# Two feed-forward blocks and an attention of a two-layer transformer: from token blocks of one batch to pairs of batches

## The chip, the cores and the metric

The kernel runs on one core of a Trainium2 chip. The metric is the device time of one execution in microseconds, as a median over runs. The engines that the text names are PE (matrix products, with PEld for its weight loads), DVE (elementwise work on vectors), ACT (elementwise functions and copies), POOL or GpSimd (elementwise work) and SP (issues DMA transfers). Each engine works through its own queue of instructions in order; semaphores make an instruction wait for one on another engine. Matrix results land in PSUM banks (128 partitions x 512 fp32), everything else is in SBUF.

## The reference

There are 4 batches of 256 tokens with 256 features, in fp32, and four residual steps, each on a layer norm of `x`:

```python
x = x + L0_attn(layernorm(x))   # 16 heads, 8 kv heads, rms norm + rope on q and k, window of 128
x = x + L0_ffn(layernorm(x))    # below
x = x + L1_attn(layernorm(x))   # 16 heads of 128, causal softmax, output projection W_O
x = x + L1_ffn(layernorm(x))    # silu(x W1) * (x W3), Walsh-Hadamard transform, then W2

# L0_ffn, hidden width 1024
h = silu(x @ w_gate) * (x @ w_up)
h_sparse = h with, of each 4 neighbours along the hidden axis, the 2 of largest |h| kept
out = h_sparse @ w_down
```

## The kernel before

Four stages follow each other on the core. In the trace the first attention takes 0 to 279 us, the first FFN 279 to 372, the second attention 372 to 655, and the second FFN 655 to the end at 737.2. A scheduler of the framework fixes the order of instructions on every engine when the program is built; tile pools (with a tag and a number of buffers each) decide when a buffer may be written again, and `tc.issue_after` puts an instruction behind another one.

**First FFN** (`ffn0`, `gated`, `keep_two_of_four`, `down`). Eight units: batch `b`, half `gc` of the hidden width. A unit has 16 plain matmuls (L550; 2 weights x 4 hidden blocks x 2 chunks of the contraction) with 256 moving columns, the batch's tokens. ACT applies Silu to the gate's PSUM tile (L556), DVE multiplies by up (L557, out of PSUM), ACT takes Abs (L530), and DVE builds the mask of the two largest and applies it (`keep_two_of_four`, L569 to L583, 256 columns wide, on bf16 counts). The down matmuls (L595) of a unit are issued two units later; the last two units' downs are done inside the second attention (`finish_ffn0`).

**Seven-product scheme** (`seven_products`, `left_of`, `right_of`). In the second attention's q, k and v projections and the second FFN's gate and up, a product of 2x2 blocks is made with seven block products instead of eight. `left_of` forms four sums of the blocks of x on DVE, `right_of` four sums of the blocks of the weights. The products come in the order 5, 1, 2, 6, 3, 7, 4 into PSUM tiles x, y, z: ACT copies the results of 5, 1 and 6 to SBUF (`u`), DVE adds c11 after 2, c12 after 3, c22 after 7 (three-way sums that use a `u`), and ACT copies c21 after 4. The lines that carry this:

```python
product(x, 6, False)
nc.scalar.copy(u[2], x)
product(y, 3, False)
nc.vector.tensor_tensor(c12, y, u[2], ALU.add)
```

Before the change the two left blocks are the two blocks of 128 tokens of one batch, so the moving operand of q, k, gate and up has 128 columns.

**Second attention** (`attention1`, `project1`, `pipelined`). 16 units of four heads (group `g`) and one batch. `pipelined` runs the stages project (unit n), score (n - 1) and attend (n - 2) in one step, and after them what `behind` holds for that step. A unit has 28 matmuls of 128 columns for q and k (L783) and 7 of 256 for v (L789), scores (L213, L214), the softmax, then GpSimd normalizes (`p`, L234) and splits it into 16-bit planes (`pl`, L240), a DMA transposes the planes (`plT`), ACT and DVE copy them together (`pT`, L260), and PE multiplies with v (`av`, L268, L271); ACT copies the result to `zT`. The output projection of unit n (`po`, L280) is behind step n + 3 for the first nine units; outputs 9, 10, 11 and 13 are `kept` and issued between the products of units 14 and 15's steps, 12 is at step 15, 14 and 15 at step 17. `load_group1` loads a group's weights by four DMAs on SP and forms `t_qk` and `t_v` on DVE; groups 0 and 1 are loaded ahead of the first FFN.

**Second FFN** (`ffn1`, `gated1`, `factors_ffn1`). Eight units of one batch and half of the hidden width, 28 matmuls of 128 columns (L858) and 8 downs of 256 of the unit before, which `between` puts among the products; `factors_ffn1` forms the weights' sums on DVE.

**Norms** (`normed`). With `by_dma` DVE makes `xn` (L171), GpSimd splits it into planes (`xpl`), a DMA on SP transposes them (`xplT`), and ACT joins them to `xnT` (L195).

## Time and profile before

| | |
|---|---|
| Median of 3 runs | 738.72 us (738.62 to 738.83) |
| Profiled execution, first to last instruction | 737.2 us |
| Median less that span | 1.5 us |
| Busy | PE 725.0, DVE 469.2, ACT 406.9, POOL 345.0 us |
| Granted PE clock | 1.00 over the span |

The profile is of one execution. The page gives the busy time of each engine, the chain of waits that ended last, and groups of instructions by source line: `Lnnn engine operation out<-in, partitions x elements, type, xcount | busy us, mean ns of one | idle us before them and what ended it`. The table by stage gives for a stretch of time the busy time (and count) of PE, PEld, DVE, ACT and POOL, the granted clock, the DMA share and GB/s. The timeline gives start, length, engine, line, operation and count; a bracket holds the idle time before and its releaser. Each fp32 matmul appears as two records, and the records of neighbouring matmuls overlap, so the rate of issue is read from the starts.

### The profile page before, as it was taken

How to read it: one execution, taken by the hardware profiler on the slowest of the kernel's cores; microseconds unless marked ns; L12 is line 12 of the kernel's file. 1: busy time of each engine (PE TensorE's matmuls, PEld its weight loads, DVE VectorE, ACT ScalarE, POOL GpSimd, SP SyncE). 2: the span in 40 equal slices, each digit the busy share in tenths (PEclk: the TensorE clock that was granted, in tenths of full speed). 3: DMA queues.
4: the chain of work that ended last, by engine and by line, in shares of the span. 5: the costliest groups of instructions: out<-in, count | busy, mean ns of one | idle time of the engine just before them, and what ended most of it. 6: DMA issues, size and time to landing. Idle time of an engine off the chain costs nothing.

```text
span 737.2 us, 11593 instructions
## 1 busy us (share of the span) xinstructions
PE 725.0 (98%) x3912; PEld 594.6 (81%) x3912; DVE 469.2 (64%) x1402; ACT 406.9 (55%) x983; POOL 345.0 (47%) x489
## 2 busy tenths in 40 slices
PE   9999999999999999999999999999999999999998
PEld 5556576666666778888898999999998999899997
DVE  6999878888887537987655644464442655464443
ACT  2487887667767952222355555555556576434332
POOL 1588878897799631011116433343336575520000
PEclk9999999999999999999999999999999999999999
DMA  8732344425445545001324532342232223401100
GB/s 327 293 64 51 57 93 81 92 52 93 90 79 96 77 114 180 16 14 26 119 72 77 127 55 44 70 129 46 44 72 44 44 44 44 88 15 22 23 14 30
DMA packets 138348, 57.51 MB, mean 78 GB/s; under 512 B 131504, under 2 KB 133680, under 8 KB 137520
## 3 DMA queue, kind: packets, MB, share of 16 engines
q1 hardware_dynamic: 138288, 56.77, 33.9%
q8 instruction: 31, 0.51, 0.3%
q14 instruction: 29, 0.24, 0.1%
HBM read 22.94 MB, written 1.05 MB: 33 GB/s over the span
## 4 chain that ended last, share of the span: by engine, by line
PE 75%; DVE 9%; POOL 7%; issue 4%; ACT 3%; DMA 2%; SPq 0%; POOLq 0%; DVEq 0%; ACTq 0%
PE pj L446 10%; PE pgu L550 7%; PE po L292 7%; PE po_f L595 7%; PE qk_x L783 5%; PE po L280 5%; PE sc L214 5%; PE gu_x L858 4%; PE av L394 3%; PE qk_y L783 3%; PE v_x L789 3%; PE sc L213 3%; PE av L268 2%; POOL p L234 2%; PE gu_y L858 2%
## 5 line engine op out<-in xcount | busy, mean ns | idle before, releaser
L234 POOL TENSOR_SCALAR p<-p,rs 128x128 f32<-128x128 f32 (+1 forms) x256 | 115.4, 470 | 153.2 <-DVE rs L231 147.9
L240 POOL TENSOR_SCALAR pl<-p 128x1536 uint16<-128x1536 uint16 x64 | 94.3, 1474 | 4.8 <-POOL p L234 0.5
L260 ACT COPY pT<-plT 128x1536 uint16<-128x1536 uint16 (+1 forms) x60 | 86.2, 1494 | 11.5 <-DMA plT<-pl 11.5
L216 DVE CUSTOM_DVE_ANT_0 p<-sc,cst 128x128 f32<-128x128 f32 (+1 forms) x256 | 79.7, 351 | 10.5 <-PE sc L214 8.1
L226 ACT ACTIVATE p<-p,nb,r 128x128 f32<-128x128 f32 (+1 forms) x128 | 68.2, 535 | 20.2 <-DVE nb L223 20.2
L446 PE MATMUL pj<-wq,xnT 128*128 128x512 f32 x128 | 61.1, 595 | 1.1 <-DVE qT L508 1.1
L446 PE MATMUL pj<-wkv,xnT 128*128 128x512 f32 x128 | 60.1, 592 | 0.0
L226 ACT ACTIVATE p<-p,nb 128x128 f32<-128x128 f32 (+1 forms) x128 | 56.3, 447 | 4.0 <-DVE nb L221 4.0
L292 PE MATMUL po<-wo,zT 128*128 128x256 f32 x256 | 57.9, 379 | 0.0
L280 PE MATMUL po<-w_o,zT 128*128 128x256 f32 x256 | 57.6, 379 | 0.0
L456 ACT ACTIVATE sq<-pj 128x512 f32<-128x512 f32 (+1 forms) x64 | 30.9, 489 | 42.7 <-DVE qc L451 42.4
L292 PEld LDWEIGHTS po<-wo,zT 128*128 128x128 f32 x256 | 48.3, 190 | 7.0 <-ACT kT L519 0.6
L280 PEld LDWEIGHTS po<-w_o,zT 128*128 128x128 f32 x256 | 47.7, 190 | 6.0
L156 POOL TENSOR_SCALAR ve<-mv 128x2 f32<-128x2 f32 (+1 forms) x17 | 4.3, 253 | 97.5 <-DVE mv L152 97.0
L446 PEld LDWEIGHTS pj<-wkv,xnT 128*128 128x128 f32 x128 | 24.3, 190 | 30.2 <-issue 28.0
L451 DVE TENSOR_TENSOR qs<-pj,sin_s 128x512 f32<-128x512 f32 (+1 forms) x64 | 35.3, 551 | 13.5 <-PE pj L446 12.9
L446 PEld LDWEIGHTS pj<-wq,xnT 128*128 128x128 f32 x128 | 23.5, 190 | 24.2 <-issue 19.9
L666 ACT COPY qk<-qk_x 128x512 f32<-128x512 f32 x16 | 9.4, 587 | 58.1 <-PE qk_x L783 58.1
L268 PE MATMUL av<-pT,v 128*128 128x256 f32 x128 | 38.4, 382 | 1.2 <-DVE nb L221 1.1
L214 PE MATMUL sc<-kT,qT 128*128 128x256 f32 x128 | 38.3, 381 | 0.0
L214 PE MATMUL sc<-qk 128*128 128x256 f32 x128 | 38.2, 380 | 0.0
L240 POOL TENSOR_SCALAR qpl<-qc 128x1024 uint16<-128x1024 uint16 x20 | 28.8, 1453 | 18.9 <-PE av L398 8.2
(151 smaller groups left out, 1748.8 us busy)
## 6 DMA issues: line engine op xcount, KB each, us to landing
w<-in_w_dram SPq DMA_DIRECT2D x3, 1024.0 KB, 4.7
wq<-in_wq_dram SPq DMA_DIRECT2D x4, 512.0 KB, 7.6
wkv<-in_wkv_dram SPq DMA_DIRECT2D x4, 512.0 KB, 8.4
wo<-in_wo_dram SPq DMA_DIRECT2D x4, 512.0 KB, 10.2
w_qk<-in_w_q_dram SPq DMA_DIRECT2D x4, 512.0 KB, 5.2
w_qk<-in_w_k_dram SPq DMA_DIRECT2D x4, 512.0 KB, 6.1
w_v<-in_w_v_dram SPq DMA_DIRECT2D x4, 512.0 KB, 7.3
w_o<-in_w_o_dram SPq DMA_DIRECT2D x4, 512.0 KB, 6.0
```

What stands on the lines that cost most here:

```text
L214: nc.tensor.matmul(sc[:, P : 3 * P], lhsT=q[:, P:T], rhs=k, start=True, stop=True)
L216: last_of["mx"] = nc.vector.tensor_tensor_reduce(out=p[:, j, cols], in0=sc[:, cols], in1=mask[:, cols], scale=1.0, scalar=-3.0e38, op0=ALU ...
L226: last_of["exp"] = nc.scalar.activation(p[:, j, cols], p[:, j, cols], AF.Exp, bias=nb[:, j, i : i + 1], scale=SCALE1 if rq is None else rq ...
L234: nc.gpsimd.tensor_scalar(p[:, j, cols], p[:, j, cols], rs[:, j, i : i + 1], 1.0, ALU.mult, ALU.mult)
L240: last_of["planes"] = nc.gpsimd.tensor_scalar(o, i, 1.0, 1.0, ALU.mult, ALU.mult)
L260: copy(words.rearrange("p (n w) -> p w n", w=2), halves[:, :, js].rearrange("p w j n -> p w (j n)"),)
L268: nc.tensor.matmul(av, lhsT=v0, rhs=pT[:, 0:T], start=True, stop=False, skip_group_check=True)
L280: nc.tensor.matmul(po[:, t, :], lhsT=zT[:, j, t * P : (t + 1) * P], rhs=w[:, j, :], start=(t == j == 0), stop=(j == 3), skip_group_check=True,
L292: nc.tensor.matmul(po, lhsT=zTs[hd // 4][:, hd % 4, t * P : (t + 1) * P], rhs=w[:, hd, :], start=(hd == 0), stop=(hd == n - 1),)
L446: last_of[0] = nc.tensor.matmul(pj, lhsT=xnT[:, c, t * P : (t + 1) * P], rhs=w[:, g, c, :], start=(c == 0), stop=(c == NC - 1),)
L550: nc.tensor.matmul(o[:, j, :], lhsT=w[:, c, f0 + j, :], rhs=xnT[:, c, :], start=(c == 0), stop=(c == NC - 1),)
L783: last_of[1] = nc.tensor.matmul(o[:, j, :], lhsT=wqk[i - 1][:, j // 2, j % 2, :], rhs=x[i - 1], start=(first and j == 0), stop=True, skip_ ...
```

## The change

Batches are taken in pairs from the first FFN on. The seven-product schemes take the two batches of a pair, rather than the two token blocks of a batch, as the rows of the left blocks: `left_of` gets two normed batches, and the moving operands have 256 columns. A unit of the second attention is then a group, a pair and a half `a` of its heads; v is made per token block `a`. The output projection of a batch needs two `zT` and stands one step later (n + 4); 13 moves to step 15, outputs 14 and 15 become fill of the second FFN's first unit.

The first FFN's gate and up are made by the scheme, in 4 units of 28 matmuls, by the same `gated` that the second FFN now uses; `factors` for it runs on GpSimd. Gate and up are SBUF tiles of the tag "qk" (2 buffers). The product h is made on GpSimd per batch, Abs on ACT per batch, and `keep_two_of_four` is 512 columns wide. The first `load_group1` is issued after the third unit, with its sums on GpSimd; the others follow in the second attention. Pools are split by stage: `work0`, `work1`, `work2`; the first FFN's norm planes have 4 buffers, h 2, a and counts 1, and `st` has 4 PSUM banks from the first FFN on.

The core of the diff:

```diff
+    def norm_planes(shape, name):
+        if in_ffn0:
+            return work.tile(shape, U16, tag="npl", name=name, bufs=4)
+        return page_of_planes(shape, name)
...
-    def project_out1(po, zT, w, b):
+    def project_out1(po, heads, w, b):
 
         for t in range(NT):
-            for j in range(4):
+            for j, zT in enumerate(heads):
                 nc.tensor.matmul(
-                    po[:, t, :], lhsT=zT[:, j, t * P : (t + 1) * P], rhs=w[:, j, :],
+                    po[:, t, :], lhsT=zT[:, t * P : (t + 1) * P], rhs=w[:, j, :],
                     start=(t == j == 0), stop=(j == 3), skip_group_check=True,
                 )
-        for t in range(NT):
+                if j % 2:
+                    yield
...
+    def factors(half, w_g, w_u, engine):
+
+        t = late.tile([P, 2, 4, 2, P], F32, tag="qkt", name="t_gu")
+        r = []
+        for i, w in enumerate((w_g, w_u)):
+            w = w[:, :, 4 * half : 4 * half + 4, :].rearrange("p c (a m) f -> p c a m f", m=2)
+            r.append(right_of(*(w[:, c, :, m, :] for c in range(2) for m in range(2)),
+                              [t[:, i, k] for k in range(4)], engine))
+        return r
+
+    def gated(x, r, gate_at, up_at, between):
+
+        def chain(w, o):
+            def product(ps, i, first):
+                for j in range(2):
+                    nc.tensor.matmul(
+                        ps[:, j, :], lhsT=w[i - 1][:, j, :], rhs=x[i - 1],
+                        start=(first and j == 0), stop=True, skip_group_check=True,
+                    )
+
+            c = o.rearrange("p (a m) b t -> p a m b t", m=2)
+            return seven_products(
+                product, st([P, 2, T], "gu_x"), bank([2, T], "gu_z"), st([P, 2, T], "gu_y"),
+                *(c[:, :, m, b, :] for b in range(2) for m in range(2)), [P, 2, T],
+            )
+
+        def fill(n):
+            for _ in range(n):
+                next(between, None)
+
+        g, u = (late.tile([P, 4, 2, T], F32, tag="qk", name=name) for name in ("gate", "up"))
+        gate, up = chain(r[0], g), chain(r[1], u)
+        for i in range(7):
+            if i == 6:
+                next(up)
+            next(gate)
+            fill(gate_at.get(i, 0))
+        nc.scalar.activation(g, g, AF.Silu)
+        for i in range(1, 7):
+            next(up)
+            fill(up_at.get(i, 0))
+            if i == 4:
+                yield g, u
+        yield g, u
+
     def ffn0():
-        hs, xn = {}, dict(enumerate(xn_f))
...
-        counts = work.tile([P, 8, T], BF16, tag="page", name="counts", bufs=8)
+        counts = work.tile([P, 8, 2 * T], BF16, tag="counts", name="counts")
...
-                ci, a[:, i : i + 1, :].to_broadcast([P, n, T]), a[:, i + 1 :, :], ALU.is_ge
+                ci, a[:, i : i + 1, :].to_broadcast([P, n, 2 * T]), a[:, i + 1 :, :], ALU.is_ge
...
-        b, gc = divmod(n, 2)
...
+        p, half = divmod(n, 2)
+        for k in range(2):
+            b = 2 * p + k
+            if half == 0:
+                pos[b] = bank([NT, D], "po_f")
+            for t in range(NT):
+                for j in range(4):
+                    nc.tensor.matmul(
+                        pos[b][:, t, :], lhsT=hs[n][k][:, j, t * P : (t + 1) * P],
+                        rhs=w[:, 4 * half + j, :], start=(half == t == j == 0),
+                        stop=(half == 1 and j == 3), skip_group_check=True,
+                    )
+                    if j == 1:
+                        yield
+                if half == 1:
+                    x = xs[b * NT + t]
+                    nc.vector.tensor_tensor(x, pos[b][:, t, :], x, ALU.add)
+                    if last:
+                        at = (b * NT + t) * P
+                        nc.sync.dma_start(out[at : at + P, :], x)
+                yield
...
-    def left_of(xnT):
-
-        s = late.tile([P, 4, P], F32, tag="xs4", name="xs4", bufs=4)
-        x11, x12, x21, x22 = (xnT[:, c, t * P : (t + 1) * P] for t in range(2) for c in range(2))
+    def left_of(x0, x1):
+
+        s = late.tile([P, 4, T], F32, tag="xs4", name="xs4")
+        x11, x12, x21, x22 = (x[:, c, :] for x in (x0, x1) for c in range(2))
         for i, a, b, op in (
             (0, x21, x22, ALU.add), (1, s[:, 0], x11, ALU.subtract),
             (2, x11, x21, ALU.subtract), (3, x12, s[:, 1], ALU.subtract),
             nc.vector.tensor_tensor(s[:, i], a, b, op)
         return x11, x12, s[:, 3], x22, s[:, 0], s[:, 1], s[:, 2]
...
-    def right_of(w11, w12, w21, w22, t):
+    def right_of(w11, w12, w21, w22, t, engine=nc.vector):
 
         for i, a, b, op in (
             (0, w12, w11, ALU.subtract), (1, w22, t[0], ALU.subtract),
             (2, w22, w12, ALU.subtract), (3, w21, t[1], ALU.subtract),
         ):
-            nc.vector.tensor_tensor(t[i], a, b, op)
+            engine.tensor_tensor(t[i], a, b, op)
         return w11, w21, w22, t[3], t[0], t[1], t[2]
...
     def attention1(finish_ffn0):
-        left = left1
+        left, vs = left1, {}
+
+        def unit(n):
+            g, n = divmod(n, 4)
+            return g, *divmod(n, 2)
 
         def project(n, _):
-            g, b = divmod(n, 4)
-            if b == 1 and 1 <= g < 3:
+            g, p, a = unit(n)
+            qk, vs[g, p, a] = project1(left[p], gw[g], a)
+            if p == 0 and a == 1 and g < 3:
                 load_group1(g + 1)
-            held = project1(left[b], gw[g])
-            if g == 0 and b + 1 < B:
+            if n == 1:
                 with tc.issue_after(last_of["sum"].ins):
-                    left[b + 1] = left_of(xn1[b + 1])
...
+                    left[1] = left_of(xn1[2], xn1[3])
+            return qk
+
+        def score(n, qk):
             ps = [
-                probabilities(qk[:, 0], qk[:, 1], (2 * kk, 2 * kk + 1), mask1) for kk in range(2)
+                probabilities(qk[:, 0, :, k, :], qk[:, 1, :, k, :], (0, 1), mask1)
+                for k in range(2)
             ]
-            return [planes(p, page_of_planes) for p in ps], v
...
+            return [planes(p, page_of_planes) for p in ps]
+
+        zTs, kept = {}, {14: (10,), 15: (11,)}
+
+        def attend(n, ps):
+            g, p, a = unit(n)
             for m in kept.get(n, ()):
                 out(m, True)(zTs)
             zTs[n] = zT = page("zT1")
-            for kk in range(2):
-                pT = joined(ps[kk], (
+            for k in range(2):
+                pT = joined(ps[k], (
                     (
                         (nc.vector.tensor_copy, slice(0, 1), None) if n < 1 else
                         (nc.scalar.copy, slice(0, 1), last_of["copy"])
                 ))
                 av = bank([2, T], "av1")
                 for j in range(2):
-                    values(v[:, 0, 2 * kk + j, :], v[:, 1, 2 * kk + j, :], pT[:, j], av[:, j, :])
-                nc.scalar.copy(zT[:, 2 * kk : 2 * kk + 2, :], av)
+                    v0, v1 = (vs[g, p, t][:, k, 2 * a + j, :] for t in range(NT))
+                    values(v0, v1, pT[:, j], av[:, j, :])
+                nc.scalar.copy(zT[:, 2 * k : 2 * k + 2, :], av)
             return zT
 
+        def product_out(n, po):
+            g, b = divmod(n, 4)
+            p, k = divmod(b, 2)
+            heads = [zTs[4 * g + 2 * p + a][:, 2 * k + j, :] for a in range(2) for j in range(2)]
+            return project_out1(po, heads, gw[g][2], b)
+
         def out(n, kept=False):
-            g, b = divmod(n, 4)
 
             def emit(done):
                 if not kept:
-                    project_out1(bank([NT, D], "po1"), done[n], gw[g][2], b)
+                    run(product_out(n, bank([NT, D], "po1")))
                 else:
                     with tc.issue_after(last_of[1].ins):
-                        project_out1(st([P, NT, D], "po1"), done[n], gw[g][2], b)
+                        run(product_out(n, st([P, NT, D], "po1")))
             return emit
 
-        behind = {n + 3: [out(n)] for n in range(9)}
+        behind = {n + 4: [out(n)] for n in range(10)}
...
-        behind.setdefault(15, []).append(out(12))
+        behind.setdefault(15, []).extend((out(12), out(13)))
         behind[16] = behind.get(16, []) + [
-            lambda _: xn_f.append(normed(0, by_dma=True)),
+            lambda _: xn_f.extend(normed(b, by_dma=True) for b in range(2)),
             prepare_ffn1(1),
         ]
-        behind[17] = [out(14), out(15)]
         pipelined((project, score, attend), (0, 1, 2), behind, (0, 1, 2))
+
+        def rest():
+            for n in (14, 15):
+                yield from product_out(n, bank([NT, D], "po1"))
+        return rest()
...
-    def project1(x, w):
+    def project1(x, w, a):
         wqk, wv, _ = w
-        qk = late.tile([P, 2, 4, T], F32, tag="qk", name="qk1")
-        v = late.tile([P, NT, 4, HD], F32, tag="v", name="v1", bufs=3)
+        qk = late.tile([P, 2, 2, 2, T], F32, tag="qk", name="qk1")
+        v = late.tile([P, 2, 4, HD], F32, tag="v", name="v1", bufs=4)
 
         def product_qk(o, i, first):
-            for j in range(4):
+            for j in range(2):
                 last_of[1] = nc.tensor.matmul(
-                    o[:, j, :], lhsT=wqk[i - 1][:, j // 2, j % 2, :], rhs=x[i - 1],
+                    o[:, j, :], lhsT=wqk[i - 1][:, j, a, :], rhs=x[i - 1],
                     start=(first and j == 0), stop=True, skip_group_check=True,
                 )
 
         def product_v(o, i, first):
             last_of[1] = nc.tensor.matmul(
-                o, lhsT=x[i - 1], rhs=wv[i - 1], start=first, stop=True, skip_group_check=True
+                o, lhsT=x[i - 1][:, a * P : (a + 1) * P], rhs=wv[i - 1], start=first,
+                stop=True, skip_group_check=True,
             )
 
-        c = qk.rearrange("p k (a m) (t c) -> p (k a) m t c", m=2, t=NT)
         products = [seven_products(
-            product_qk, *(st([P, 4, P], f"qk_{n}") for n in "xzy"),
-            *(c[:, :, m, t, :] for t in range(2) for m in range(2)), [P, 4, P],
+            product_qk, *(st([P, 2, T], f"qk_{n}") for n in "xzy"),
+            *(qk[:, :, m, b, :] for b in range(2) for m in range(2)), [P, 2, T],
...
-    def ffn1():
...
+    def ffn1(before):
+        hs, left = {}, {0: left_of(xn_f[0], xn_f[1])}
+        for n in range(4):
+            p, half = divmod(n, 2)
+            if n:
+                before = down(hs, n - 1, w2h[0], last=True)
+            hs[n] = []
+            done = 0
+            for g, u in gated(
+                left[p], r_ffn1[half], {3: 1, 5: 1, 6: 1} if n else {3: 1, 4: 1, 5: 1, 6: 1},
+                {2: 1, 3: 1, 4: 1, 5: 2}, before,
+            ):
+                h = page("h1")
+                nc.vector.tensor_tensor(h, u[:, :, done, :], g[:, :, done, :], ALU.mult)
+                hs[n].append(h)
+                done += 1
+            run(before)
+            if n == 0:
+                xn = {b: normed(b, by_dma=True) for b in range(2, 4)}
+            if n == 1:
+                left[1] = left_of(xn[2], xn[3])
+        run(down(hs, 3, w2h[0], last=True))
...
-    ps2_open, ps2 = open_pool("ps2a", bufs=2, space=PSUM)
+    work_open.close()
+    work_open, work = open_pool("work1", bufs=1)
+    st_open, st_pool = open_pool("st", bufs=4, space=PSUM)
     late = ctx.enter_context(
         tc.tile_pool(name="late", bufs=2, reuse_waits="tile", side="right")
     )
-    load_group1(0)
-    load_group1(1)
-
+
+    in_ffn0 = True
     finish_ffn0 = ffn0()
-    xn_f.clear()
-    ps2_open.close()
+    in_ffn0 = False
+    work_open.close()
+    work_open, work = open_pool("work2", bufs=1)
     w1_sb = load_ffn(w1, (NC, NF, P), "w1")
     w3_sb = load_ffn(w3, (NC, NF, P), "w3")
     w2_raw = load_ffn(w2, (NF, D), "w2")
-    st_open, st_pool = open_pool("st", bufs=4, space=PSUM)
-    attention1(finish_ffn0)
-    ffn1()
+    ffn1(attention1(finish_ffn0))
     st_open.close()
+    work_open.close()
```

## The prediction

> **What bounds the kernel now.** I read the page first (busy row, slices, shares of the chain), then a table of busy time by stage, then groups by shape, then PE's timeline. Page:
>
> ```profile
> PE 725.0 (98%) x3912; PEld 594.6 (81%) x3912; DVE 469.2 (64%) x1402; ACT 406.9 (55%) x983; POOL 345.0 (47%) x489
> ...
> PEclk9999999999999999999999999999999999999999
> ...
> PE 75%; DVE 9%; POOL 7%; issue 4%; ACT 3%; DMA 2%; SPq 0%; POOLq 0%; DVEq 0%; ACTq 0%
> ```
>
> PE is busy 725.0 of 737.2 us at full clock: only fewer matmul columns or new PE stalls can move the time much. The table by stage (PE, PEld, DVE, ACT, POOL; clock, DMA share, GB/s):
>
> ```profile
> 279.00:372.00 93.00, 92.57 (x457) 81.94 (x457) 72.07 (x191) 25.92 (x34) 11.17 (x18) 1.00 0.21 61
> ...
> 414.00:561.00 147.00, 147.00 (x961) 136.79 (x961) 69.04 (x255) 80.10 (x232) 55.82 (x86) 1.00 0.31 62
> 561.00:655.00 94.00, 93.88 (x578) 84.98 (x577) 50.62 (x186) 52.35 (x142) 54.66 (x75) 1.00 0.31 54
> ```
>
> The first FFN (279 to 372) and the second attention are gapless on PE: there is no stall to recover, and every stall the change creates is added whole.
>
> **What a matmul costs.** Each is two records. PE's timeline:
>
> ```profile
> 278.83 3.62 PE L550 MATMUL pgu<-xnT,w_gate 128*128 128x256 f32 x16
> 282.28 3.62 PE L550 MATMUL pgu<-xnT,w_up 128*128 128x256 f32 x16
> ...
> 655.05 1.05 PE L858 MATMUL gu_y<-xs,t_gu 128*128 128x128 f32 x8
> ```
>
> Eight matmuls of 256 columns take 282.28 - 278.83 = 3.45, so 0.432 us each. Four of 128 take 0.89 by the chain (656.10 to 657.00), 0.224 each: two cost 0.448. Widening saves 0.016 a pair, no more.
>
> **PE's sum without stalls.** First FFN: straight, 8 units x 16 = 128 matmuls; seven-product, 4 x 28 = 112. 16 x 0.432 = -6.9; the 64 downs stay. Attention 1: 16 units x 14 pairs x 0.016 = -3.6 (0.2 of it beside the last downs, so -3.3 for 15 units behind them). Second FFN: 112 pairs, -1.8. Total -12.2 us.
>
> **What that buys on the other engines** in one pair unit of the first FFN:
>
> ```profile
> L830 POOL TENSOR_TENSOR w_b<-w 128x512 f32<-128x512 f32 x8 | 10.6, 1354 | 1.5 <-ACT w L820 1.5
> L557 DVE TENSOR_TENSOR h<-pgu,s 128x1024 f32<-128x1024 f32 x8 | 9.7, 1218 | 5.9 <-PE pgu L550 5.9
> L569 DVE TENSOR_TENSOR counts<-a 128x768 bf16<-128x768 f32 x8 | 7.6, 954 | 5.0 <-ACT a L530 5.0
> L583 DVE SCALAR_TENSOR_TENSOR h<-counts,h 128x256 f32<-128x256 bf16 x32 | 12.0, 414 | 0.0
> L651 ACT COPY u<-qk_x 128x512 f32<-128x512 f32 x16 | 9.4, 586 | 5.5 <-PE qk_x L783 5.3
> L530 ACT ACTIVATE a<-h 128x1024 f32<-128x1024 f32 x8 | 8.5, 1057 | 36.0 <-DVE h L557 36.0
> ```
>
> Groups by shape; the number after the busy time is the mean ns. DVE: six c sums of 128x512 at 0.60 start to start (row L663: 690 ns) = 3.6, plus keep_two_of_four at double width. A single one takes 4.77 on the timeline (1.9 counts, 8 half sums at 0.20, 4 h at 0.335); doubled, columns scale (L569 954/683/416 ns for 768/512/256): 3.4 + 2.7 + 2.4 = 8.5. ACT: eight copies at 0.48, a silu 128x2048 (1.9: two of row L556, 1.02), a table load 1.28, two Abs at 1.05: about 9. PE: 28 x 0.432 + 16 x 0.432 = 19.0. GpSimd: the moved h mult. Before shows no 128x1024 tensor-tensor there; L830 gives 1.35 to 1.44 for half of it (also 0.657 for 256 columns, L492), so 2.7 each, two a unit. Bounds: 1.2 (the DVE row L557) and 3.3 (2.7 lengthened by contention). I take 2.7, as L830 is the same engine and operation. factors on GpSimd add 8 x 0.66 = 5.3 per half. No engine exceeds PE's 19, so throughput is not the problem; order is.
>
> **Where PE waits.** I laid the queues of the built changed program out by hand, T = 0 at the first gate matmul (278.83 before). Two orders bite. On ACT, Abs of h stands ahead of u copies that the next unit's products wait for, and Abs waits for GpSimd. On DVE, the 8.5 us of keep_two_of_four stands ahead of the next c12 and c22 sums, whose banks (4 in st) PE needs. gate and up have two buffers, so the next c11 also waits for the second h.
>
> - Unit 0 to 1: h of the second batch ends at T = 21.4; up's product 6 waits for a copy behind its Abs: 1.25. The first down waits for keep_two's first result at 28.0: 2.0.
> - Unit 1 to 2: silu ends 35.75, h at 38.5 and 41.2, Abs 42.3, copy 42.8; PE is ready for gate's product 7 at 39.05: 3.8.
> - Unit 2 to 3: t_qk of load_group1 (128x512, 1.4) stands between the two h mults on GpSimd; h ends 62.7: 3.0. c11 of unit 3's up lies behind keep_two (to 72.35) and the norm's xn: 1.8 at 73.3, then 0.75 and 0.7 (xnT copies).
> - Unit 3 to attention: copies behind the last Abs: 1.55 and 0.6; pieces under 0.5 make some 2.5.
>
> Sum about 18. Unit 0's start is put at nothing: left_of and factors(0) lie beside attention 0's last output projections; cost if uncovered, up to 2. The point where the first FFN's downs and project unit 0 are done lies at 371.68 - 278.83 = 92.85 before, and at T = 103.85 by this: 198 matmuls x 0.432 = 85.5 + 18.3. So instead of gaining 6.9 this stage loses 11.0, of which 0.4 is a v matmul that only comes earlier: +10.6. The moved load_group1(0) issues four DMAs, 5 to 7 us each to landing (page, DMA issues); they stand on SP ahead of a norm's transposition that is not yet ready, at no cost. Its eight right_of instructions leave DVE for GpSimd: four t_v of 0.66 before unit 0's h has its inputs, four t_qk of 1.4, one of which is priced above. The planes of later norms behind h on GpSimd are covered by downs, except the 1.55.
>
> A page bears on the h term: the Trainium skill, "GPSIMD Engine Reference", section 3.1, times a GpSimd tensor-tensor add of 2048 fp32 at 4497 ns; by proportion an estimate of 2.25 for 1024, with which the total below would be 3 us lower. No run here shows that size.
>
> Contention is in the trace: two sums L582, 0.48 elsewhere, take 1.31 while GpSimd splits xn (DVE's timeline, GpSimd's xpl 301.25 to 302.60):
>
> ```profile
> 301.43 1.31 DVE L582 TENSOR_TENSOR counts<-counts 128x256 bf16<-128x256 bf16 x2
> ```
>
> In units 0 and 2 keep_two can meet GpSimd's planes or t_qk: 0 to 5 us, taken 0. The skill's page "SBUF — State Buffer", section "Who interferes with whom", speaks against this change: a DVE instruction with two SBUF inputs contends with a GpSimd one reading SBUF, and the later one blocks whole; all of keep_two has two.
>
> **Attention 1.** Steady units keep PE fed (ACT and DVE had half their time free); out one step later costs nothing until the end. The first pT comes up to 2 us late: +0.7. The end, before:
>
> ```profile
> 629.13 6.64 PE L280 MATMUL po<-w_o,zT 128*128 128x256 f32 x30
> ...
> 638.23 7.07 PE L280 MATMUL po<-w_o,zT 128*128 128x256 f32 x32
> 645.14 0.59 PE L268 MATMUL av<-pT,v 128*128 128x256 f32 x2
> ```
>
> From the last score (629.13) 31 po matmuls and av(14) fill 16.0 us, and pT(15) arrives at 641.89 + 1.06, 13.8 us after the score. After the change out(14) and out(15) are fill in the second FFN and 22 po stand before the last scores; behind them stay 4 po + av(14) + 6 po = 6.9 us. The pT chain (softmax, p 1.6, planes 1.5, transposition 3.7, copy 1.06) is unchanged: 11 to 13.8, the second half 14 to 17.6. Stall 3 to 9, taken 5.
>
> **Second FFN.** -1.8, plus some 1.3 where xnT copies and a 1.9 silu stand ahead of a u copy on ACT in its second unit: -0.5 (from -1.8 to +0.5).
>
> **Sum:** 10.6 - 3.3 + 0.7 + 5 - 0.5 = +12.5 on the span 737.2, so 749.7. The median 738.72 lies 1.5 above the span: 751.2. Bounds: h at 1.2 takes 1.5 for each mult off the stalls that end with h, at most 1.25 + 2.0 + 3.0 + 1.5 + 1.55 = 9.3 (742); h at 3.3 adds 0.6 for each of some seven, 4; the end at 3 or 9 moves it by -2 or +4 (759 at most, 740 at least).
>
> **Rivals.** *Faster:* the chains are shorter than laid out and PE stays fed, 738.72 - 12.2 = 726.5. It decides where silu to copy fits PE's 3.3 us of cover in unit 1: with Abs and copy 1.6, h at 0.85. Against it: L830. For it: GpSimd is idle then, and a lay-out by hand can miss overlap. Half way, h at 1.2 and the end at 3 with the 1.8 at T = 73.3 hidden too, gives 751.2 - 9.3 - 2 - 1.8 = 738. Chance of faster 0.26. *Worse:* keep_two meets GpSimd's reads as in L582 above and the end is at its upper bound: 751.2 + 5 + 4 = 760 and up; 0.12. *The change is not what it says* (throughput on PE falls short): 256 columns at 0.432 are in the trace, so no. My forecast's own case, 740 to 759: 0.59; the half way around 738: 0.03 as no change. 0.2%, 1.5 us, is what a measurement can tell. So slower 0.71. The range 729 to 764 leaves out the fully hidden case at 726.5 and the far worse end, some 2 in 10.
>
> **What the profile after would show.** PE idle of 15 to 20 us between 279 and 385, brackets naming ACT's u copies and DVE's sums and keep_two; GpSimd's h mult at 2.7; DVE's doubled h row near 0.7; units of attention 1 at 17.74 rather than 17.97; 3 to 9 us idle ahead of the last av; the second FFN some 1 us shorter. I am wrong if h takes near 1.2, if Abs turns out not to hold the copies, or if the last av follows at once.

## The result, and the profile after

| | before | after |
|---|---|---|
| Median | 738.67 us (738.58 to 738.83) | 766.02 us (765.51 to 766.36) |
| Profiled execution | 737.2 us | 763.7 us |

The ratio is 1.0369 (95% interval 1.0354 to 1.0384): 27.3 us slower, where the forecast was 12.5 slower with a range up to 764. The page of the kernel after, busy row, granted clock by slices and shares of the chain:

```profile
PE 726.4 (95%) x3204; PEld 565.4 (74%) x3204; DVE 475.3 (62%) x1341; ACT 423.5 (55%) x1007; POOL 385.0 (50%) x523
...
PEclk9999999999999999999999999999999999989999
...
PE 59%; DVE 11%; POOL 11%; issue 7%; ACT 6%; DMA 4%; SPq 0%; POOLq 0%; DVEq 0%; ACTq 0%
```

There are 708 matmul records fewer (3912 to 3204), most of them because one matmul now has the columns of two, and yet PE's busy time is not shorter (725.0 to 726.4), and 37 us of the span are idle instead of 12. PE's share of the chain falls from 75 to 59%; DVE, GpSimd (POOL) and waits of issue fill the rest. The table by stage of the kernel after (columns as before: PE, PEld, DVE, ACT, POOL, clock, DMA share, GB/s):

```profile
279.00:390.00 111.00, 94.26 (x401) 76.09 (x400) 77.61 (x142) 42.95 (x62) 36.78 (x30) 0.97 0.18 52
...
430.00:680.00 250.00, 243.08 (x1207) 212.22 (x1205) 120.10 (x440) 137.68 (x387) 109.86 (x160) 0.99 0.29 58
```

Both stretches differ from before in kind: in the first FFN PE is idle for 16.7 us and its clock is 0.97; in attention 1 with its end PE is idle for 7 us and the clock is 0.99. Stage by stage, start to start on PE's timeline (forecast in brackets): up to the first gate product -0.4 (0); from there to the last down 110.28 instead of 92.85, +17.4 (+11.0); from the last down to the second FFN's first product +8.8, counting the 16 output matmuls that moved into the second FFN as 6.9 (+2.0: 0.7 + 5 - 3.3, less the 0.4 of the v matmul that comes earlier); the second FFN +0.65 (-0.5). Sum +26.5, the difference of the spans.

PE's timeline of the first FFN in the kernel after, the larger waits (the bracket holds the idle time before and its releaser):

```profile
296.63 1.13 PE L542 MATMUL gu_x<-xnT,t_gu 128*128 128x256 f32 x4 [1.55 <-DVE up L719]
302.51 1.10 PE L542 MATMUL gu_x<-xs,t_gu 128*128 128x256 f32 x4 [0.73 <-ACT u L707]
307.57 0.67 PE L651 MATMUL po_f<-w_down,h 128*128 128x256 f32 x2 [1.66 <-issue]
321.58 1.64 PE L542 MATMUL gu_x<-xs,t_gu 128*128 128x256 f32 x4 [2.87 <-ACT u L713]
344.16 1.13 PE L542 MATMUL gu_x<-xs,t_gu 128*128 128x256 f32 x4 [2.06 <-ACT u L707]
353.36 1.73 PE L651 MATMUL po_f<-w_down,h 128*128 128x256 f32 x6 [1.25 <-DVE h L637]
356.54 1.13 PE L542 MATMUL gu_x<-xs,t_gu 128*128 128x256 f32 x4 [1.45 <-ACT u L707]
369.68 1.89 PE L851 MATMUL qk_y<-xs,t_qk 128*128 128x256 f32 x4 [4.08 <-DVE xs L687]
```

The forecast's waits for u copies are there and somewhat shorter (2.87 for 3.8, 2.06 for 3.0, 0.73 for 1.25). The third is the first down's wait for keep_two_of_four (2.0 in the forecast). The first, the sixth and the last line were not forecast. What stands behind these three is on the timelines of DVE and GpSimd:

```profile
293.38 2.58 DVE L687 TENSOR_TENSOR xs<-xnT 128x256 f32<-128x256 f32 x2 [0.46 <-ACT xnT L197]
295.89 0.68 DVE L719 TENSOR_TENSOR up<-gu_x,u 128x512 f32<-128x512 f32 x1
...
343.18 5.64 DVE L623 TENSOR_TENSOR counts<-a 128x1536 bf16<-128x1536 f32 x3 [4.26 <-ACT a L595]
...
362.37 5.50 DVE L696 TENSOR_TENSOR t_qk<-w_qk 128x512 f32<-128x512 f32 x2 [1.22 <-PE gu_x L542]
367.80 1.40 DVE L696 TENSOR_TENSOR t_qk<-w_qk,t_qk 128x512 f32<-128x512 f32 x2
```

```profile
293.00 2.35 POOL L594 TENSOR_TENSOR h<-up,gate 128x1024 f32<-128x1024 f32 x1 [5.43 <-DVE up L716]
...
343.23 2.83 POOL L696 TENSOR_TENSOR t_qk<-w_qk 128x512 f32<-128x512 f32 x1
...
362.21 2.35 POOL L594 TENSOR_TENSOR h<-up,gate 128x1024 f32<-128x1024 f32 x1 [3.38 <-ACT gate L564]
364.98 2.35 POOL L594 TENSOR_TENSOR h<-up,gate 128x1024 f32<-128x1024 f32 x1 [0.42 <-ACT up L722]
```

Two t_qk sums take 1.40 when they run alone, and two of the same size 5.50 beside GpSimd's two h. They are those of `load_group1(1)`, and on DVE they stand ahead of the sums xs that attention 1's first product waits for. The first wait is alike: two sums xs take 2.58 beside GpSimd's h, and the sum of up (L719) that PE waits for stands behind them. Ahead of the sixth, the counts take 5.64 beside GpSimd's t_qk, and so the masked h of the downs comes late. The end of attention 1, PE and DVE of the kernel after:

```profile
650.17 3.72 PE L282 MATMUL po<-w_o,zT 128*128 128x256 f32 x16 [2.08 <-DVE x L289]
...
668.27 1.22 PE L270 MATMUL av<-pT,v 128*128 128x256 f32 x2 [3.54 <-ACT pT L262]
```

```profile
649.22 0.60 DVE L262 COPY pT<-plT 128x768 uint16<-128x768 uint16 x1 [3.25 <-DMA plT<-pl]
649.71 0.41 DVE L289 TENSOR_TENSOR x<-po,x 128x256 f32<-128x256 f32 x1
```

The 3.54 is the forecast's wait for pT. The 2.08 is another one: DVE waits 3.25 for a transposed plane, and the sum x that frees the bank of the next output projection stands behind that copy.

### The profile page after: what moved, and what is told of

Its sections match the earlier page's. It is cut to its first block, busy times and chain, and to the rows that moved or that the text cites. A ratio compares the mean times of both kernels' runs of the same rounds, so it can differ in the third digit from the quotient of the medians.

```text
span 763.7 us, 10177 instructions
## 1 busy us (share of the span) xinstructions
PE 726.4 (95%) x3204; PEld 565.4 (74%) x3204; DVE 475.3 (62%) x1341; ACT 423.5 (55%) x1007; POOL 385.0 (50%) x523
## 4 chain that ended last, share of the span: by engine, by line
PE 59%; DVE 11%; POOL 11%; issue 7%; ACT 6%; DMA 4%; SPq 0%; POOLq 0%; DVEq 0%; ACTq 0%
PE pj L449 10%; PE po L295 7%; PE gu_x L542 5%; PE po_f L651 5%; PE po L282 4%; PE sc L216 4%; PE qk_x L851 4%; POOL p L236 3%; PE av L397 3%; POOL pl L242 3%; PE gu_y L542 2%; PE sc L215 2%; DMA plT<-pl 2%; ACT p L228 2%; DVE p L218 2%
## 5 line engine op out<-in xcount | busy, mean ns | idle before, releaser
L282 PE MATMUL po<-w_o,zT 128*128 128x256 f32 x256 | 60.9, 381 | 2.8 <-DVE x L289 2.8
L270 PE MATMUL av<-pT,v 128*128 128x256 f32 x128 | 40.4, 399 | 4.5 <-ACT pT L262 3.9
L542 PE MATMUL gu_x<-xs,t_gu 128*128 128x256 f32 x128 | 35.7, 402 | 8.4 <-ACT u L707 5.5
L594 POOL TENSOR_TENSOR h<-up,gate 128x1024 f32<-128x1024 f32 x8 | 18.8, 2349 | 43.0 <-ACT gate L564 34.1
```

The costliest lines, as they stand in the source:

```text
L270: nc.tensor.matmul(av, lhsT=v0, rhs=pT[:, 0:T], start=True, stop=False, skip_group_check=True)
L282: nc.tensor.matmul(po[:, t, :], lhsT=zT[:, t * P : (t + 1) * P], rhs=w[:, j, :], start=(t == j == 0), stop=(j == 3), skip_group_check=True,)
L542: nc.tensor.matmul(ps[:, j, :], lhsT=w[i - 1][:, j, :], rhs=x[i - 1], start=(first and j == 0), stop=True, skip_group_check=True,)
```

## The experiments

Theory: first-FFN waits come from h on GpSimd, by its latency and by what it does to DVE; the end from outputs placed ahead of the last scores; the start of attention 1 from group 1's sums. Rivals: the clock, and the scheme's queues whatever engine h is on. Ratios are to the kernel before; "less" and "more" are against the kernel after, 766.02, where nothing else is said.

**e1_warm.** Filler matmuls, whose results are overwritten, keep PE busy ahead of two of the three places where the clock fell (the third is behind the wait of 2.87).

```diff
+            if fill and i == 5:
+                for _ in range(9): nc.tensor.matmul(o[:, 0, :], lhsT=wqk[0][:, 0, a, :], rhs=x[0], ...)
...
+                for _ in range(8 if n == 15 and k == 0 else 0): nc.tensor.matmul(av[:, 0, :], ...)
```

> The changed kernel with 17 extra matmuls of 256 columns whose results are overwritten: nine ahead of the first projection of attention 1 and eight ahead of the last unit's product with v, where PE stood idle for 4.08 and 3.54 us. No wait is taken away. Theory (PE's granted clock halves after a long idle and costs about 1.6 us behind the first and 2.5 us behind the second of these two): clock 1.00 in those places and about 762.0 us. Rival (those matmuls were slow because operands came late, or the clock has another reason): 766 us as before, or up to 7 us more if the extra matmuls add to the path.

Measured 768.34, 1.0393 (1.0378 to 1.0409). In the kernel after the windows of 2 us show it (columns as in the table by stage):

```profile
370.00:372.00 2.00, 2.00 (x6) 1.56 (x5) 1.97 (x3) 0.39 (x1) 0.00 (x0) 0.50 0.00 0
...
668.00:670.00 2.00, 1.73 (x5) 1.55 (x6) 1.46 (x3) 0.21 (x1) 1.62 (x2) 0.50 1.10 209
```

With the filler, from the same view of e1_warm:

```profile
370.00:372.00 2.00, 2.00 (x11) 1.76 (x10) 2.00 (x2) 1.14 (x3) 0.00 (x0) 1.00 0.00 0
...
668.00:670.00 2.00, 1.14 (x6) 0.70 (x5) 1.05 (x3) 0.48 (x1) 0.67 (x1) 1.00 1.09 204
```

The clock is 1.00 at both, and no time is gained (2.3 more): PE waits 1.66 for DVE at 378.81 and 1.45 and 1.73 at 670.63 and 673.93 instead. At these two places the half clock ran inside other waits. The third place was left as it was; by the starts of its matmuls it costs 1.8. The clock is no large part of the 27 us.

**e2_group1_late.** Group 1's sums stand behind the last sum of the second projection unit.

```diff
-                load_group1(g + 1)
+                with tc.issue_after(last_of["sum"].ins) if g == 0 else nullcontext():
+                    load_group1(g + 1)
```

> The changed kernel with the sums of the second weight group (t_qk, t_v on DVE) put behind the last sum of the second projection unit, so that the left sums xs of attention 1 no longer stand behind them. Theory (the 4.08 us wait comes from DVE's t_qk, two of which took 5.50 us beside GpSimd's h instead of 1.40): the wait falls to under 0.7 us and the slow clock behind it goes, together -5 us, about 761. Rival (xs waits for the copied xnT anyway, so only the contention moves to another place): 765 to 766.

Measured 762.29, 1.0316 (1.0299 to 1.0333), 3.7 less. The wait of 4.08 is gone; 1.03 for a u copy is left in that place.

**e3_end.** Outputs 10 to 13 behind the last scores instead of ahead of them. The norm of batch 1 reads `x` there before output 13 is added.

```diff
-        zTs, kept = {}, {14: (10,), 15: (11,)}
+        zTs, kept = {}, {14: (10, 11, 12), 15: (13,)}
...
-                    with tc.issue_after(last_of[1].ins):
+                    with tc.issue_after(last_of["sc"].ins):
...
-        behind.setdefault(15, []).extend((out(12), out(13)))
```

> The changed kernel with the output projections of batches 10 to 13 (numbered by unit) issued behind the last score products instead of partly ahead of them. Theory (at the end of attention 1 the last planes are late because 22 matmuls and a 2.08 us wait stand ahead of the last scores and only 10 are left as cover): of 6.8 us idle between 648 and 672 and 2.8 us lost to the clock, 8 us go, about 758. Rival (the banks of these projections are released by DVE sums that stand behind the same late copies, so the wait only moves): 763 or more.

Measured 763.35, 1.0328 (1.0313 to 1.0344), 2.7 less. PE's larger waits at the end are now both for x: 1.82 at 650.53 and 2.44 at 666.62. Fill alone helps little while the sums that free its banks stand on DVE behind its half of pT, or, for the second of these, behind an xn.

**e4_h_dve.** h on DVE.

```diff
-                nc.gpsimd.tensor_tensor(h[:, :, b, :], u[:, :, b, :], g[:, :, b, :], ALU.mult)
+                nc.vector.tensor_tensor(h[:, :, b, :], u[:, :, b, :], g[:, :, b, :], ALU.mult)
```

> The changed kernel with the first FFN's product h on DVE instead of GpSimd, nothing else. Theory (the chain silu, h, Abs, copy and the contention between DVE's two-input sums and GpSimd's h make most of the 16.6 us idle of PE in the first FFN): h takes 1.2 instead of 2.35 us, DVE's xs pair 0.75 instead of 2.58 and its t_qk pair 1.4 instead of 5.5; 8 to 12 us less, 754 to 758. Rival (DVE becomes the queue that PE waits for, with 2.4 us more per unit ahead of keep_two's results and the next sums): 763 to 769.

Measured 753.75, 1.0200 (1.0175 to 1.0224), 12.3 less by one word; its four runs lie between 751.80 and 755.98. The groups by shape, first of after, then of e4_h_dve:

```profile
L594 POOL TENSOR_TENSOR h<-up,gate 128x1024 f32<-128x1024 f32 x8 | 18.8, 2349 | 43.0 <-ACT gate L564 34.1 <-DVE up L716 5.4 <-ACT up L722 3.5
```

```profile
L594 DVE TENSOR_TENSOR h<-up,gate 128x1024 f32<-128x1024 f32 x8 | 11.0, 1397 | 3.4 <-ACT gate L564 3.3
```

In the profiled execution (751.80, the fastest) the first FFN to its last down takes 96.15 instead of 110.28. That is still 3.3 more than the straight one's 92.85, with eight waits of 0.24 to 1.89 left, so the scheme's queues cost more than its columns save even with the faster h.

**e5_straight.** The first FFN of before, with the first two groups' weight sums ahead of it on DVE as there, and pairs from the second attention on.

```diff
-            *_, (g, u) = gated(left[p], r[half], ...)
...
+        for n in range(8):
+            b, gc = divmod(n, 2)
+            hs[n] = h = gated0(xn[b], gate_sb, up_sb, 4 * gc, "h")
```

> The changed kernel with the first FFN as it was before (straight products, 256-wide masks, h on DVE, both first weight groups' sums ahead of it on DVE), and pairs from attention 1 on. Theory (of the 26.5 us on the profiled span, the stage from the first gate product to the last down of the first FFN holds 17.4): about 749 us, above before by the end of attention 1 alone. Rival (pairs cost time in attention 1's steady part or the second FFN, or the first FFN's loss is made up later): 756 or more, or under 742.

Measured 747.60, 1.0124 (1.0109 to 1.0140): 18.4 of the 27.3 are the first FFN's scheme and the start of attention 1 behind it.

**e6_end_act.** The end: outputs 12, 13, 10, 11 behind the last scores, and both halves of the last two pT on ACT, so that no sum of x stands behind a plane on DVE.

```diff
-                    (nc.vector.tensor_copy, slice(1, 2), last_of["sum"]),
+                    (nc.vector.tensor_copy if n < 14 else nc.scalar.copy, slice(1, 2),
+                     last_of["sum"]),
```

> The changed kernel with the output projections of units 12, 13, 10, 11 in this order behind the last score products, and both halves of the last two units' pT copies on ACT, so that DVE's sums that release the banks do not stand behind copies that wait for a transposition. Theory (end of attention 1: late scores and DVE sums behind late pT copies): the 6.8 us of idle between 648 and 672 fall to under 2, 7 to 8 us less, about 758. Rival (the norm of the next stage or the transposition itself then binds): 761 or more.

Measured 758.48, 1.0269 (1.0255 to 1.0283), 7.5 less. **e7_straight_end_act** joins it with e5's first FFN.

> Both: the straight first FFN and the end of attention 1 as in the kernel before it in this call. Theory (two independent losses; what stays is wider matmuls in attention 1, 3.4 us, and in the second FFN, 1.8 us): 734 to 738, below before. Rival (pairs cost in the steady part or the second FFN): 741 or more.

Measured 740.96, 1.0035 (1.0022 to 1.0048). At the end of attention 1 both have one wait above 1 us left, of 2.48, for a sum x that stands on DVE behind an xn waiting for GpSimd's rstd.

**e8_ladder.** The clock by itself: blocks of 40 matmuls with idle gaps of 0.26 to 5.5 us between them, twice through.

> A measurement by itself, which computes no layer: 25 blocks of 40 fp32 matmuls of 256 columns (17 us each), between which PE waits for a chain of 0 to 11 DVE instructions, each size twice. Theory (the granted clock halves after an idle time of PE, only from some length between 1.5 and 4 us on, and stays so for some 3 to 5 us of matmuls): gaps under 1.5 us leave 1.00, gaps over 4 us always give near 0.5 for 3 to 5 us. Rival (the slow matmuls after the long waits are a matter of late operands): 1.00 after all gaps.

It was run once. PE's timeline of e8_ladder, parts of it (start, length of the block, and in the bracket the gap before it):

```profile
103.88 17.50 PE L64 MATMUL ps<-a,x 128*128 128x256 f32 x80 [1.79 <-DVE a L69]
123.64 19.11 PE L64 MATMUL ps<-a,x 128*128 128x256 f32 x80 [2.25 <-DVE a L69]
...
166.16 17.50 PE L64 MATMUL ps<-a,x 128*128 128x256 f32 x80 [3.18 <-DVE a L69]
187.30 19.19 PE L64 MATMUL ps<-a,x 128*128 128x256 f32 x80 [3.64 <-DVE a L69]
...
379.98 17.50 PE L64 MATMUL ps<-a,x 128*128 128x256 f32 x80 [2.26 <-DVE a L69]
...
422.45 19.19 PE L64 MATMUL ps<-a,x 128*128 128x256 f32 x80 [3.18 <-DVE a L69]
```

17.50 is the block at full clock. No gap up to 1.80 slowed the block behind it, each of 3.6 and more did, by 1.4 to 2.9, and gaps of 2.25, 2.7 and 3.2 did so once in two. The slow stretch is at 0.50 for some 3 us (28 to 31 after the gap that ends at 27.84). In a whole kernel a shorter wait was enough; PE's timeline of e2_group1_late:

```profile
296.86 1.68 PE L542 MATMUL gu_x<-xnT,t_gu 128*128 128x256 f32 x4 [1.55 <-DVE up L719]
```

The same four records behind the same wait take 1.13 in the kernel after (at 296.63); here the clock is 0.50 from 298.3 to 299.6.

**e11_square.** a = h * h on DVE in the place of Abs on ACT, h still on GpSimd: is it the order on ACT that costs?

```diff
-                nc.scalar.activation(a[:, :, b, :], h[:, :, b, :], AF.Abs)
+                nc.vector.tensor_tensor(a[:, :, b, :], h[:, :, b, :], h[:, :, b, :], ALU.mult)
```

> The changed kernel with a made as h times h on DVE in place of Abs on ACT (the same order of sizes, so the same mask), h still on GpSimd. Theory (GpSimd's time for h, and whoever stands behind it, is what costs; Abs on ACT is only the place where the wait shows): the wait moves to DVE, whose sums c11 and c12 now stand behind h, 766 to 774. Rival (it is ACT's order, Abs ahead of the u copies, that costs, as the prediction's lay-out of ACT has it): the waits with ACT's u as releaser, 0.73, 2.87, 2.06 and 1.45 us, go and the kernel takes 757 to 761.

Measured 774.48, 1.0486 (1.0471 to 1.0501), 8.5 more. PE's timeline of e11_square, two of its waits:

```profile
334.41 1.13 PE L542 MATMUL gu_x<-xnT,t_gu 128*128 128x256 f32 x4 [3.14 <-DVE gate L719]
...
358.32 4.62 PE L651 MATMUL po_f<-w_down,h 128*128 128x256 f32 x10 [5.84 <-DVE x L660]
```

The waits of 2.87, 2.06 and 1.45 for u copies are gone (one of 1.88 is left, at 304.16), and longer ones for DVE have come: whichever engine has the instruction that waits for h at its head holds up what PE needs. The order on ACT alone is not the cause, since the rival's 757 to 761 did not come. The 8.5 is not the price of the order on DVE alone either: DVE has eight products more here, and at 2.15 each (1.21 where one ran alone) they too meet GpSimd's h.

**e10_h_g1_end3** and **e12_half_g1_end3.** h on DVE (in e12 only the second batch's), group 1 late, pT as in e6, outputs 9 to 13 behind the last scores, 14 and 15 as a block behind those, the first pair's norms a step later.

```diff
+                (nc.vector if b else nc.gpsimd).tensor_tensor(h[:, :, b, :], ...)   # e12; e10: nc.vector
...
+        zTs, kept = {}, {14: (9, 10, 11, 12, 13)}
...
+        behind[17] = [
+            lambda _: xn_f.extend(normed(b, by_dma=True) for b in range(2)), out(14), out(15),
+        ]
```

> The changed kernel (seven-product first FFN kept) with h on DVE, the second weight group's sums late, and the same end of attention 1. Theory (the single fixes add up as far as they touch other waits: 12.3 for h, 1 to 2 of the 3.7 for the weight group because h no longer runs beside it, 9 to 11 for the end): 741 to 745, still above before because keep_two_of_four's first result is late for the downs. Rival (the waits were one chain and the fixes overlap): 748 or more.

> As the second kernel of this call, but h of the first batch of each pair on GpSimd and only that of the second batch on DVE. Theory (only the last h before Abs and the copies is on the path; the first one can run while up's last sums are made): within 2 us of that kernel, and better if DVE's load is what is left. Rival (contention of GpSimd's h with DVE's two-input sums counts too): 3 to 6 us above it.

Measured 745.67, 1.0091 (1.0078 to 1.0104), and 750.32, 1.0160 (1.0147 to 1.0173): half of the h mults on GpSimd cost 4.7. In e12 GpSimd has one h at a time, and DVE's timeline gives the same instruction alone and beside it; below it GpSimd's own:

```profile
298.69 1.23 DVE L595 TENSOR_TENSOR h<-up,gate 128x1024 f32<-128x1024 f32 x1 [1.05 <-ACT up L723]
...
314.92 3.01 DVE L595 TENSOR_TENSOR h<-up,gate 128x1024 f32<-128x1024 f32 x1 [2.72 <-ACT up L723]
```

```profile
314.49 2.36 POOL L595 TENSOR_TENSOR h<-up,gate 128x1024 f32<-128x1024 f32 x1 [18.86 <-ACT gate L565]
```

GpSimd's ends at 316.85, and DVE's, which began second, 1.08 after that.

**e9_straight_end3.** The same end with the straight first FFN.

> The straight first FFN, pairs from attention 1 on, and an end of attention 1 laid out for cover: the output projections of units 9 to 13 all behind the last scores, both halves of the last pT copies on ACT, those of 14 and 15 as one block ahead of the second FFN as before, and the norms of the next stage issued behind DVE's sums. Theory (pairs save 3.4 us of matmul time in attention 1 and up to 1.8 in the second FFN once the end has cover; the 2.48 us wait left in the run before came from DVE's norm standing ahead of the sums): 734 to 738, under before. Rival (the pair form itself costs something in the second FFN and the start that eats the saving): 739 to 742.

Measured 743.99, 1.0068 (1.0054 to 1.0083): a miss, 3 above e7. The end is gapless (626 to 655, PE busy 29.00 of 29), but two waits are new. PE's timeline of e9_straight_end3:

```profile
613.78 1.13 PE L875 MATMUL qk_x<-xs,t_qk 128*128 128x256 f32 x4 [1.87 <-ACT u L740]
...
685.29 1.13 PE L546 MATMUL gu_x<-xs,t_gu 128*128 128x256 f32 x4 [2.08 <-ACT u L734]
```

Output 9, taken away from its step, had covered a u copy behind zT; and the second pair's norms now lie so late that ACT waits for their planes ahead of a u copy. In this execution half clock follows both: after the first a group of 4 records takes 1.77 instead of 1.03. It is the longest of the six: two with a mean clock of 1.000 took 741.93 and 742.58, two with 0.995 took 745.55 and 745.62.

**e13_straight_end4**, **e14_straight_end3_norms**, **e15_h_g1_end4.** e13 and e14 change e9, and e15 changes e10: output 9 is back behind its step (e13, e15), and the second pair's norms stand ahead of the second FFN's first unit (all three).

```diff
+        zTs, kept = {}, {14: (10, 11, 12, 13)}
...
         hs, left = {}, {0: left_of(xn_f[0], xn_f[1])}
+        xn = {b: normed(b, by_dma=True) for b in range(2, 4)}
```

> The straight first FFN and the end of the ninth experiment, with two things put right that its trace names: output 9 stands behind its own step again (its trace waits 1.87 us at 613.78 for a u copy where output 9 was missing, and the matmuls after it then run at half clock), and the norms of the second pair stand ahead of the second FFN's first unit (there DVE had xn behind the first h, the planes came late and ACT held a u copy behind them: 2.08 us at 685.29, again with half clock after it). Theory, order is all that is left: 743.99 less 1.87 and 1.6 of slow clock, less 2.08 and 1.7, plus up to 1.5 at the end, where four outputs fill 13.8 us instead of five 17.3: 736.7 to 738.3, that is as fast as the kernel before or a little faster. Rival, the pairs themselves cost what they save (longer queues in front of every wait): each wait moves on to the next late operand, 740 to 743.

> The ninth experiment with only the second pair's norms ahead of the second FFN's first unit; output 9 stays behind the last scores. Theory: the wait of 2.08 us at 685.29 and the slow clock after it go, 743.99 - 3.8 = 740.2, and the wait of 1.87 us at 613.78 stays with its slow clock. Rival: the norms' xn of the second pair, now ahead of the first unit's sums on DVE, hold those up instead: 742 to 744.

> The tenth experiment (scheme in the first FFN, h on DVE, group 1's sums late) with the same two things put right. It has the wait of 1.85 us at 620.62 too, but no long one in the second FFN. Theory: 745.67 - 1.85 (no slow clock follows it there) + up to 1 at the end = 743.5 to 745; its distance to the straight first FFN with the same end (4 to 7 us) is what the scheme in the first FFN still costs with its h on DVE, against the 6.9 us of matmul columns that it saves. Rival: no distance, both within 1 us, if the scheme only suffered from its surroundings.

Measured 739.92 (1.0013; 1.0004 to 1.0022), 741.80 (1.0043; 1.0030 to 1.0055) and 745.14 (1.0087; 1.0074 to 1.0101). e9's loss was the two misplaced pieces: back to within 1.2 of before. With the same end the scheme in the first FFN still costs 5.2 (745.14 - 739.92) with h on DVE. One wait above 1 us is left in e13 from the first FFN on, of 1.71 at 665.63, and ACT's timeline of e13_straight_end4 tells why:

```profile
663.36 1.25 ACT L200 COPY xnT<-xplT 128x512 uint16<-128x512 uint16 x2 [1.13 <-DMA xplT<-xpl]
664.51 0.58 ACT L749 COPY gate<-gu_x 128x512 f32<-128x512 f32 x1
664.99 0.59 ACT L734 COPY u<-gu_x 128x512 f32<-128x512 f32 x1
```

The u copy that PE needs is third in a queue whose head waits for a DMA.

**e16_straight_end6** and **e17_straight_end5.** In both, those xnT copies stand behind the first unit's last c21 copy; in e17 the outputs also have the order 12, 13, 10, 11.

```diff
+            if n == 0:
+                with tc.issue_after(last_of["copy"].ins):
+                    x = xn[2](), xn[3]()
+                left[1] = left_of(*x)
```

> The thirteenth experiment with one more step: the copies that join the second pair's xnT on ACT stand behind the first unit's last c21 copy, instead of ahead of a u copy that the next products wait for (its trace: 1.71 us at 665.63, while ACT waits for the planes until 663.36). Theory, order is all that is left: 739.92 - 1.71 = 738.2, no slower than the kernel before. Rival: the wait moves on to the silu and its table load, which stand behind the same products (ACT is busy to 668.7 in that trace): 739.5 to 740.5.

> The same with the four outputs behind the last scores in the order 12, 13, 10, 11, so that the first pair's norms end earlier and the 0.91 us ahead of the second FFN's sums go. Theory: 738.2 - 0.9 = 737.3. Rival: as in the seventh experiment xn then stands on DVE ahead of the sums that free the banks and waits for GpSimd's rstd: + 1.5 to 2.5, 739.7 to 740.7.

Measured 738.34, 0.9994 (0.9985 to 1.0003), and 741.05, 1.0030 (1.0020 to 1.0041). The page of e16_straight_end6:

```profile
PE 722.9 (98%) x3236; PEld 571.1 (78%) x3236; DVE 466.3 (63%) x1381; ACT 410.4 (56%) x983; POOL 344.2 (47%) x491
```

The waits above 1 us from 270 on are gone, and the kernel is level with the one before, not faster. From the last down of the first FFN to the second FFN's first product, counted alike, it gains 2.0 (281.4 against 283.4); the second FFN loses 1.4 (83.6 against 82.15), with waits of 0.85, 0.52 and 0.21 in it and the rest not traced. e17 has the wait of 2.44 for x behind xn again, as e7.

## Why the prediction was wrong

The direction was right, and so was the main mechanism: no engine's throughput, but what stands ahead of what. The size was short by 14.8. By stages these are 6.4 in the first FFN (+17.4 for +11.0), 6.8 from there to the second FFN (+8.8 for +2.0), 1.2 in the second FFN (+0.65 for -0.5) and 0.8 between span and median, less 0.4 at the start. By its own steps:

- *PE's sum without stalls, -12.2* (its terms add to 12.3). The matmuls were saved as said: 16 fewer in the first FFN, and in the other two stages half as many of the 128-column ones, now with 256. But the best arrangement tried for the pairs alone, which should give 5.1, returns nothing that a measurement can tell (e16).
- *h at 2.7 on GpSimd.* Measured 2.35. The price put on "h at 1.2", 9.3 less, was near what e4 gave, 12.3 less; but with h on DVE the contention beside it goes as well, so the 12.3 is not for the shorter h alone.
- *Waits in the first FFN, "sum about 18"* (the list adds to 17.95; 18.3 is used). The brackets of the trace add to 16.6, so the sum looks right, but by luck: most of the laid-out waits came shorter, and three unforeseen ones (1.55, 1.25, 4.08) filled the gap. Counted from starts, as the forecast counts, the 198 matmuls at 0.432 are 85.5 of the 110.28, and the rest is 24.7 instead of 18.3: the 16.6, 3.6 of half clock behind the waits of 2.87 and 4.08 (1.8 each), and 4.5 of starts further apart than 0.432. About half of the 4.5 stands at the waits themselves, since a bracket begins only at the end of the last matmul; the rest I did not separate.
- *"0 to 5 us, taken 0" for contention.* This is the step that failed most clearly. The text had the row (1.31 for 0.48) and a rule that spoke against the change, named the instructions at risk as keep_two_of_four's, and took nothing. Of keep_two_of_four the counts of one unit took 5.64 beside GpSimd's t_qk (3.50 in e12_half_g1_end3 at 319.05). But xs (2.58 for the 0.75 of e10_h_g1_end3 in the same place) and t_qk (5.50 for 1.40) lay beside h and were not looked at. The waits behind these three are 0.27 and 1.25, 1.55, and 4.08: 7.2 together, the last by its place in the queue as well. No run varies contention alone: e10 against e12 prices half the h mults on GpSimd, latency and contention together, at 4.7.
- *The first attention 1 product.* load_group1(1)'s sums on DVE ahead of xs were overlooked: the wait is 4.08, and e2 gives 3.7 back.
- *The end of attention 1, "taken 5".* This term was too small: counted from starts, PE loses 10.4 between 625 and 674. The wait for pT is 3.54 + 0.38, inside the forecast's 3 to 9. Not foreseen were the waits for banks, 2.08 + 0.23 + 0.52, the first of them because a sum of x stands behind DVE's half of pT, and half clock from about 667 to 673. e6 gives 7.5 back.
- *The clock* was left out. After e1 that omission costs little where other waits follow anyway; in e9, where none followed, it does count: some 3 us lie between its executions at a mean clock of 1.000 and those at 0.995.
- *Attention 1's units*: 17.8 a unit for the forecast's 17.74.

The rival "faster" needed silu to copy to fit PE's cover; e4 takes GpSimd's latency away and is still 15 slower than before, and e15, with the end mended too, 6.4, so it was not close. The rival "worse" (760 and up) came nearest in the number, but only in part by its reasons: keep_two met GpSimd in one unit, the wait for pT stayed below its upper bound, and xs, group 1's sums (3.7 by e2) and the waits for banks were not in it.

## What to carry to other kernels

On a kernel whose bottleneck engine has no gaps, a scheme that trades products for sums pays in queue order. List for each new elementwise instruction what stands behind it on its engine, and which of those the bottleneck waits for; do so at the seams between stages too, not only inside the new loop. If the moved work goes to GpSimd, price it twice, by its own duration and by what two-input DVE instructions beside it become. When a fix moves a wait instead of removing it, look at the head of the queue that the releaser stood in.

## What the runs showed of the hardware

- DVE and GpSimd beside each other: one DVE product of 128x1024 fp32 took 1.23 alone and 3.01 beside GpSimd's own (2.36), ending 1.08 after it (e12_half_g1_end3); two t_qk sums took 1.40 and 5.50; GpSimd's t_qk rose from 1.27 to 2.83 as well. The Trainium skill, "SBUF — State Buffer", section "Who interferes with whom", has the shared port pair as an exclusive lock; these rows agree with it, and give the price.
- The half clock: no gap up to 1.8 us brought it on in e8_ladder, each from 3.6 on did, and from 2.25 to 3.2 it came in three of six; it costs 1.4 to 2.9 us of the block behind. The Trainium skill, "TensorE: Matmul & The Clock Gate", section "HAM oscillation — how this bites in real kernels", warns of idle gaps over some 3.4 us; here 2.25 was enough, in e9_straight_end3 1.87, and in e2_group1_late 1.55, which left the clock at 1.00 in the kernel after. Why the same gap does it once and not the next time was not tested.
- GpSimd's product of 128x1024 fp32 takes 2.35, between the forecast's 2.7 and the 2.25 estimated from the Trainium skill, "GPSIMD Engine Reference", section 3.1.
